# A hand-ordered attention and feed-forward block on one core: four edits to the order of its instructions

## The chip, the cores and the metric

The kernel runs on one core of a Trainium2 chip. The metric is the device time of one execution in microseconds (us). Times of several executions are given as their median; the profile is one further execution that the hardware profiler recorded.

The engines that matter here: PE (TensorE) multiplies matrices into PSUM, PEld is its weight load; DVE (VectorE) does elementwise work and reductions; ACT (ScalarE) does activations and copies; POOL (GpSimd) does elementwise work on SBUF and issues the transfers of raw weights; SP issues the other transfers. Each engine takes its instructions strictly in the order in which the program issues them.

## What is computed

The input x has 4 batches of 512 tokens with 512 features. Cut to what matters, in plain form:

```
q = rotary(x @ Wq + bq)            # 16 heads of 32
k = rotary(x @ Wk + bk); v = x @ Wv + bv      # one head, shared by all 16
x = layernorm(x + softmax(q k' / sqrt(32)) v @ Wo + bo)
w1, w2, w3 = round(w / mean|w|) clipped to -1, 0, 1
x = layernorm(x + (sigmoid(x w1') * (x w2')) w3')     # inner width 1408 = 11 * 128
```

All in 32-bit floats, to about that precision. Where the kernel uses the faster float32r multiplication it keeps a value as two halves, a rounded head and the rest (the tail), and multiplies both.

## The kernel before

**Work and its tiles.** A batch is cut into 4 quarters of 4 heads (`c`), and each quarter's attention into 4 chunks of 128 keys (`t`). That gives 64 attention steps `n = (b, c, t)`. A step issues the scores `ps` (8 matmul records of q and k, and 4 that add the negated row maxima `negm`), the exponentials `es` on ScalarE, the product `acc` with v of the step before, and for batch 0 the sums `den`; for later batches POOL adds the exponentials up in `total`, and `den` is formed once for a quarter. Row maxima are found 7 steps ahead (`LEAD`): `pmax` on PE, then the reduction `mx` on DVE; `spread` transposes them (`pm`), negates them (`m`), writes them to memory (`rows`) and reads them back spread over partitions (`negm`).

**The order.** Everything is pinned to program order. Around the fixed parts of a step the function `Fill` draws pieces of other work from generators: `project_in` (k, v and q of a batch, a half of 4 matmul records a piece), `project_out` (the output projection, the layernorm and the transposes `pt` into the feed-forward's input `y`) and `feed_forward`. Each piece yields its length in us; `draw` takes pieces until the step's pace is used up. A yield of 0 means "not yet", and the other list is asked. Small jobs that come later wait in the list `late`, each with the slot from which its next piece may go; `due` walks that list in order, two times a step, and so the order of the list is the order of those pieces on each engine, SP's transfers among them.

**The opening** (`now < 0`, the first 48 us): the projections of batch 0, the maxima of the first 7 steps and, at its end, k of batch 1. The rotation of q and k is done by `turn` (line 229). In its form `apart`, ScalarE copies the biased product to SBUF (`r`), DVE forms `a` (product with the cosine), and the generator pauses; its second half (shuffle, product with the sine, sum) is issued when the piece after it is drawn, and the sum for the last 32 partitions is POOL's. In the other form everything is issued at once, on DVE, and the shuffle and the sine's product work in place in the PSUM tile (`pk`, `pq`). Before, batch 0 uses the first form and every other batch the second.

**The feed-forward** runs over 11 slices `f` of the inner width, cut into parts of up to 4 slices. For a slice, `gate` issues 8 matmuls `gu` and the tanh `th`; then 8 matmuls `gu` again, DVE's product `hw`, and, after the next pause, `split`: ScalarE's head `h0` and DVE's tail `h1` (both called `h` in the profile). At the end of a part the products `po` with the third weight follow, 4 chunks `t` of tokens, 2 matmuls for each slice, and DVE adds each to `xt`. All parts but a batch's last have the next part's first `gate` between the last `hw` and the first `po`. In a batch's last part the layernorm's statistics (`st`, `mv`) follow each chunk, and the chunks alternate with the next batch's transposes `pt`, whose results ScalarE and DVE take out as `y`. The last part has 3 slices for batches 0 to 2 and 4 for batch 3. This alternation is called the handover below; there are three.

**Buffers.** The products `gu`, `po`, `pt`, `pq`, `pk`, `pm` share two PSUM buffers (tag `mm`), so each has to be read out before the next but one may start. The scores `ps` and the maxima's `pmax` share two others (tag `sc`).

Of the kernel before, what the change touches and what calls it, by code (L numbers as in the profile page):

```python
# [9 lines left out]
F32 = mybir.dt.float32  # L10
F32R = mybir.dt.float32r
# [3 lines left out]
ALU = mybir.AluOpType  # L15
# [4 lines left out]
P = 128  # L20
# [7 lines left out]
def postln_block(  # L28
# [16 lines left out]
    B, T, D = x.shape  # L45
    NC = D // P
    NT = T // P
    NF = wf.shape[1]
# [9 lines left out]
    hp = ctx.enter_context(tc.tile_pool(name="hp", bufs=8))  # L58
# [5 lines left out]
    ps_mm = ctx.enter_context(tc.tile_pool(name="ps_mm", bufs=2, space=PSUM))  # L64
# [188 lines left out]
    def project_in(b):  # L253

        s = batches[b]
        n = P - HD
        while now < NC * NT * (b - 2):
            yield 0

        pk = ps_mm.tile([P, T], F32, tag="mm", name="pk")  # L260
        for c in range(NC):
            mm(pk, wkv_sb[:, c, :], s.xT[c], c == 0, c == NC - 1)
            if c == 1:
                yield -1.8
        kv = work.tile([P, T], F32, tag="kv", name="kv", bufs=1)
        act.activation(kv[n:P], pk[n:P], AF.Identity, bias=bkv_sb[n:P, 0:1])
        s.kT = work.tile([P, T], F32, tag="kT", name="kT", bufs=3)
        rotation = turn(
            [(s.kT[0:n], slice(0, n)), (s.kT[n:P], slice(0, HD))],
            pk, bkv_sb[:, 0:1], bkv_sb[:, 1:2], n, b == 0,  # L270
        )
        next(rotation)
        yield 1.8
        next(rotation, None)
        if b > 0:
            late.append((slot + 2, split_k(b)))
        for c in range(NC):

            while b + 1 == B and c + 2 >= NC and not batches[0].projected:
                yield 0  # L280
            pq = ps_mm.tile([P, T], F32, tag="mm", name="pq")
            for d in range(NC):
                mm(pq, wq_sb[c][:, d, :], s.xT[d], d == 0, d == NC - 1)
                if d == 1:
                    yield -1.8
            if b == 0:

                if c == 0:
                    room = work.tile([P, NC, T], F32, tag="y0", name="room", bufs=1)
                q = s.q[c] = room[:, c, :]  # L290
            else:
                q = work.tile([P, T], F32, tag="q", name="q")
            rotation = turn(
                [(q, slice(0, P))], pq, bq_sb[:, c : c + 1], bq_sb[:, NC + c : NC + c + 1], P, b == 0
            )
            next(rotation)
            if c == 0:
                pv = ps_mm.tile([P, NT, HD], F32, tag="mm", name="pv")
                for t in range(NT):
                    transpose(pv[:, t, :], kv[n:P, ts(t, P)], ident[n:P, n:P])  # L300
                s.v = work.tile([P, NT, HD], F32, tag="v", name="v", bufs=3)
                act.copy(s.v, pv)
            if b > 0:
                late.append((slot + 2, store_q(b, c, q)))
                s.done = c + 1
            yield 1.8
            next(rotation, None)
            s.done = c + 1
        load_xT(NC if b == 0 else 2)

# [9 lines left out]
    def store_q(b, c, q):  # L320
        q2 = work.tile([P, 2, T], F32R, tag="q2", name="q2")
        halves(q2[:, 0, :], q2[:, 1, :], q)
        yield
        whole = dram.tile([P, T], F32, tag="qw", name="qw", bufs=B * NC)
        parts = dram.tile([NG, 2, HD, T], F32R, tag="qp", name="qp", bufs=B * NC)
        move(whole, q)
        for i in range(NG):
            move(
                parts[i].rearrange("n r t -> r n t").bitcast(F32), q2[ts(i, HD)].bitcast(F32)
            )  # L330
        batches[b].qd[c] = (whole, parts)
        yield
# [196 lines left out]
    def split(head, tail, whole):  # L529

        act.copy(head, whole)
        dve.tensor_tensor(tail, whole, head.bitcast(F32), ALU.subtract)
# [41 lines left out]
    def feed_forward(b):  # L574

        s = batches[b]
        mv = small.tile([P, NT, 2], F32, tag="mv2", name="mv2")
        after = [(m, f) for f in range(NF) for m in range(2)][3:]

        short = NF % 4 if b + 1 == B else 0  # L580
        ends = sorted({0, NF, *range(short, NF, 4)})
        parts = [range(*pair) for pair in zip(ends, ends[1:])]
        w3 = [[] for _ in parts]
        th = {}

        def product(k, m):
            w = s.w.pop(0).rearrange("p (c m) -> p c m", c=NC)
            if after:
                s.w.append(load_weight(*after.pop(0)))
            if len(w3[k]) < len(parts[k]):  # L590
                w3[k].append(load_weight(2, parts[k][len(w3[k])]))
            g = ps_mm.tile([P, T], F32, tag="mm", name="gu")
            for c in range(NC):
                for i, part in enumerate(s.y):
                    mm(g, w[:, c, :], part[:, c, :], c == 0 and i == 0, c == NC - 1 and i == 1)
            return g

        def gate(k, f):

            th[f] = work.tile([P, T], F32, tag="th", name="th")  # L600
            act.activation(th[f], product(k, 0), AF.Tanh, scale=0.5)
            if b + 1 == B and f + 1 == NF:

                root = small.tile([P, 1], F32, tag="row", name="root")
                act.activation(root, eps_t, AF.Sqrt)

        for k, fs in enumerate(parts):
            h = []
            for f in fs:
                if f not in th:  # L610
                    gate(k, f)
                    yield 1.9
                up = product(k, 1)
                hw = work.tile([P, T], F32, tag="hw", name="hw")
                dve.scalar_tensor_tensor(hw, th[f], 1.0, up, ALU.add, ALU.mult)
                s.y_done = f == NF - 1
                yield 1.9
                h.append([hp.tile([P, T], F32R, tag="h", name=f"h{i}") for i in range(2)])
                split(*h[-1], hw)
            if fs[-1] + 1 < NF:  # L620
                gate(k + 1, fs[-1] + 1)
                yield 1.9
            for t in range(NT):

                while fs[-1] + 1 == NF and b + 1 < B and 0 <= batches[b + 1].transposed <= t:
                    yield 0
                po = ps_mm.tile([P, D], F32, tag="mm", name="po")
                for n, w in enumerate(w3[k]):
                    for i in range(2):
                        mm(  # L630
                            po,
                            h[n][i][:, ts(t, P)],
                            w,
                            n == 0 and i == 0,
                            n == len(fs) - 1 and i == 1,
                        )
                dve.scalar_tensor_tensor(s.x[t], po, 0.5, s.x[t], ALU.mult, ALU.add)
                if fs[-1] + 1 == NF:
                    stats(s.x[t], mv, t)
                    if b + 1 == B:  # L640
                        for done in range(max(t - 1, 0), t if t + 1 < NT else NT):
                            for _ in layernorm(s.x[done : done + 1], mv[:, done : done + 1, :], True):
                                pass
                            late.append((slot + 1, store(b, done)))
                    elif t == NT - 1:
                        late.append((slot + 1, layernorm(s.x, mv)))
                yield 0.24 * 2 * len(fs)
        if b + 1 < B:
            for t in range(NT):
                late.append((slot + 6, store(b, t)))  # L650
# [58 lines left out]
    late = []  # L709
    slot = 0  # L710
# [21 lines left out]
    def find_maxima(k, *chunks):  # L732

        if k >= len(steps):
            return
        b, c, i = steps[k]
        if chunks[0] == 0:
            ask(k + HEADS)
            while batches[b].done <= c or (b and k not in heads):
                if batches[b].done <= c:  # L740
                    fill.one()
                else:
                    due()
                    ask(k)
        if b == 0:
            row_maxima(b, c, i, chunks[0] // 2)
        else:
            maximum(b, c, i, chunks, heads[k])
        if i == NG - 1 and chunks[-1] == NT - 1:
            late.append((slot + (1 if now < 0 else 2), spread(b, c)))  # L750

    def feed(b):
        fill.urgent.append(project_out(b))
# [122 lines left out]
```

## Time and profile before

| what | value |
|---|---|
| three executions | 702.5, 702.6, 697.24 us; median 702.5 |
| profiled execution | 699.91 us, its span 698.1 us |
| PE busy | 668.9 us, 96% of the span |
| DVE, ACT, POOL busy | 394.0, 290.1, 323.6 us |
| mean granted TensorE clock | 0.986 of full speed |
| chain that ended last | PE 84%, DVE 8%, DMA 2%, ACT 2%, issue 2%, POOL 1% |

The span runs from the first to the last instruction; 1.8 us of the execution lie around it. The granted clock is the share of its full speed at which TensorE was allowed to run. "Waits" are told as engine, waiting instruction, and what ended the wait, with the total in us, the number and the longest.

### The profile page before, as it was taken

The numbers are of one execution on the slowest core, as the hardware profiler recorded it, in microseconds if no ns is written. First come the engines' busy times: TensorE is split into PE (matmuls) and PEld (weight loads), VectorE is DVE, ScalarE is ACT, GpSimd is POOL, SyncE is SP. The second block draws the span as 40 slices with busy tenths as digits, with TensorE's granted clock in tenths as the row PEclk, the third lists the DMA queues.
The fourth block names the chain that finished last, engine by engine and source line by source line (L and its number), as shares of the span: only waits on it lengthen the run. The fifth ranks groups of instructions, "written<-read, shape, count | busy, mean of one in ns | idle before, by whom it ended". The sixth has DMA issues, their size and how long they took to land.

```text
span 698.1 us, 9545 instructions
## 1 busy us (share of the span) xinstructions
PE 668.9 (96%) x3318; PEld 362.2 (52%) x3318; DVE 394.0 (56%) x570; ACT 290.1 (42%) x453; POOL 323.6 (46%) x413
## 2 busy tenths in 40 slices
PE   8989999999979999999999999999998999999995
PEld 6323333443323345665456565654455676768884
DVE  1885676587846675655555764555534433454435
ACT  2454646555424554434334445243434431224213
POOL 0623333435888694657555373666573812202000
PEclk9997999999999999999999999999999999999998
DMA  8662767488648258446213338351130474235631
GB/s 281 242 217 59 239 192 243 134 284 277 197 135 253 93 164 264 121 131 175 77 51 105 113 122 253 93 182 44 52 101 24 137 220 142 68 113 180 191 112 61
DMA packets 59663, 107.20 MB, mean 154 GB/s; under 512 B 13664, under 2 KB 14176, under 8 KB 59616
## 3 DMA queue, kind: packets, MB, share of 16 engines
q1 hardware_dynamic: 51696, 80.65, 37.7%
q0 software_dynamic: 7920, 25.96, 11.3%
q8 instruction: 26, 0.43, 0.3%
q14 instruction: 21, 0.17, 0.1%
HBM read 83.76 MB, written 22.81 MB: 153 GB/s over the span
## 4 chain that ended last, share of the span: by engine, by line
PE 84%; DVE 8%; DMA 2%; ACT 2%; issue 2%; POOL 1%; SPq 1%; ACTq 0%; DVEq 0%; POOLq 0%
PE gu L79 24%; PE po L79 19%; PE ps L79 12%; PE pmax L79 8%; PE acc L79 8%; PE pq L79 6%; PE den L79 4%; DVE mx L74 3%; PE pk L79 1%; DVE xt L74 1%; PE warm L79 1%; ACT es L74 1%; DMA rden<-flat 1%; POOL total L74 1%; DMA xt<-in_x 1%
## 5 line engine op out<-in xcount | busy, mean ns | idle before, releaser
L74 DVE TENSOR_REDUCE mx<-pmax 128x1 f32<-128x512 f32 (+1 forms) x159 | 158.6, 1009 | 113.5 <-PE pmax L79 113.3
L74 ACT ACTIVATE es<-ps 128x1024 f32<-128x1024 f32 x128 | 124.2, 1022 | 154.5 <-PE ps L79 154.5
L79 PE MATMUL gu<-y,wg 128*128 128x512 f32 x704 | 173.2, 395 | 1.3 <-DVE xt L74 0.7
L79 PEld LDWEIGHTS gu<-y,wg 128*128 128x128 f32 x704 | 130.9, 188 | 40.5 <-issue 6.9
L74 POOL TENSOR_TENSOR total<-total,es 128x512 f32<-128x512 f32 x96 | 123.6, 1319 | 47.1 <-ACT es L74 47.1
L79 PE MATMUL po<-wd,h 128*128 128x512 f32 x352 | 90.5, 402 | 6.1 <-DVE h L74 2.6
L74 POOL TENSOR_TENSOR total<-es 128x512 f32<-128x512 f32 x48 | 60.5, 1291 | 69.4 <-ACT es L74 69.4
L79 PEld LDWEIGHTS po<-wd,h 128*128 128x128 f32 x352 | 65.5, 190 | 29.2 <-DVE xt L74 4.3
L79 PE MATMUL pmax<-kr,qr 128*128 128x512 f32 x192 | 75.0, 453 | 2.2 <-ACT es L74 1.6
L79 PE MATMUL acc<-es,v 128*32 128x512 f32 x512 | 68.2, 605 | 0.0
L79 PEld LDWEIGHTS pmax<-kr,qr 128*128 128x128 f32 x192 | 33.7, 188 | 56.1 <-issue 21.4
L74 DVE SCALAR_TENSOR_TENSOR hw<-th,gu 128x512 f32<-128x512 f32 x44 | 30.3, 688 | 56.6 <-PE gu L79 54.9
L74 ACT CAST h<-hw 128x512 fp32r<-128x512 f32 x44 | 27.3, 622 | 82.0 <-DVE hw L74 81.9
L74 DVE SCALAR_TENSOR_TENSOR xt<-po,xt 128x512 f32<-128x512 f32 x48 | 33.2, 692 | 49.7 <-PE po L79 49.6
L79 PE MATMUL ps<-negm,ones_r 2*128 2x512 f32 x256 | 59.0, 787 | 2.0 <-DMA negm<-rows 2.0
L79 PE MATMUL po<-wo_sb,ctxT 128*128 128x512 f32 x128 | 59.1, 594 | 0.3 <-DVE hw L74 0.3
L74 POOL DMA_DIRECT2D raw<-in_wf x66 | 36.1, 549 | 49.0 <-DMA w<-raw 28.2
L74 DVE TENSOR_TENSOR h<-hw,h 128x512 fp32r<-128x512 f32 x44 | 42.6, 968 | 26.3 <-ACT h L74 25.9
L79 PE MATMUL ps<-qT,kT 32*128 32x512 f32 x384 | 55.7, 640 | 0.0
L79 PE MATMUL pq<-xT,wq_sb 128*128 128x512 f32 x112 | 53.0, 601 | 1.0 <-ACT v L74 1.0
L74 ACT ACTIVATE th<-gu 128x512 f32<-128x512 f32 x44 | 26.3, 598 | 45.5 <-PE gu L79 45.4
L79 PEld LDWEIGHTS po<-wo_sb,ctxT 128*128 128x128 f32 x128 | 23.9, 189 | 23.5 <-issue 21.1
(93 smaller groups left out, 630.3 us busy)
## 6 DMA issues: line engine op xcount, KB each, us to landing
wg<-w SPq DMA_DIRECT2D x88, 256.0 KB
raw<-in_wf POOLq DMA_DIRECT2D x66, 256.0 KB, 4.8
qr<-qp SPq DMA_DIRECT2D x96, 128.0 KB
wd<-w SPq DMA_DIRECT2D x44, 256.0 KB
w<-raw POOLq DMA_DIRECT2D x33, 256.0 KB, 4.9
qp<-q SPq DMA_DIRECT2D x48, 128.0 KB
rden<-flat SPq DMA_DIRECT2D x64, 64.0 KB
xt<-in_x SPq DMA_DIRECT2D x16, 256.0 KB
```

What stands on the lines that cost most here:

```text
L74: return lambda *args, **kw: pin(getattr(self.engine, name)(*args, **kw))
L79: pin(nc.tensor.matmul(out, lhsT=lhsT, rhs=rhs, start=start, stop=stop))
```

## The change

Four edits.

1. **Rotation.** `turn` takes the form `apart` whenever it is called in the opening (`now < 0`) and not only for batch 0. Since q may then not be complete before the pause, `store_q` is put on the list after the pause, for the slot after the one in which the generator resumes, and not before it for the slot after the next; `s.done` is set after the pause only.
2. **Heads.** The tiles for a slice's `h` are allocated before the pause. For the last slice of a part ScalarE's head is issued at once behind `hw`; for the others after the pause, as before. The tail is issued after the pause in each case.
3. **Chunks in twos.** In a batch's last part the first two chunks are one piece: the matmuls of all slices but the last for both, then those of the last slice for both, then for each chunk the sum and the statistics. The other two chunks are single as before. The piece waits until two of the next batch's transposes have been issued, where the first chunk waited for one; its length is yielded as that of two.
4. **Maxima's transfers.** `spread` is put at the front of `late`, and so its transpose and its transfers `rows` and `negm` go ahead of whatever else is due in the same slot.

```diff
-            pk, bkv_sb[:, 0:1], bkv_sb[:, 1:2], n, b == 0,
+            pk, bkv_sb[:, 0:1], bkv_sb[:, 1:2], n, now < 0,
...
-                [(q, slice(0, P))], pq, bq_sb[:, c : c + 1], bq_sb[:, NC + c : NC + c + 1], P, b == 0
+                [(q, slice(0, P))], pq, bq_sb[:, c : c + 1], bq_sb[:, NC + c : NC + c + 1], P, now < 0
...
-            if b > 0:
-                late.append((slot + 2, store_q(b, c, q)))
-                s.done = c + 1
             yield 1.8
             next(rotation, None)
+            if b > 0:
+                late.append((slot + 1, store_q(b, c, q)))
             s.done = c + 1
...
+                h.append([hp.tile([P, T], F32R, tag="h", name=f"h{i}") for i in range(2)])
+                if f == fs[-1]:
+                    act.copy(h[-1][0], hw)
                 yield 1.9
-                h.append([hp.tile([P, T], F32R, tag="h", name=f"h{i}") for i in range(2)])
-                split(*h[-1], hw)
+                if f < fs[-1]:
+                    act.copy(h[-1][0], hw)
+                dve.tensor_tensor(h[-1][1], hw, h[-1][0].bitcast(F32), ALU.subtract)
...
-            for t in range(NT):
-                while fs[-1] + 1 == NF and b + 1 < B and 0 <= batches[b + 1].transposed <= t:
+            ahead = NT // 2 if fs[-1] + 1 == NF else 1
+            for some in [range(ahead)] + [(t,) for t in range(ahead, NT)]:
+                while fs[-1] + 1 == NF and b + 1 < B and 0 <= batches[b + 1].transposed <= some[-1]:
                     yield 0
-                po = ps_mm.tile([P, D], F32, tag="mm", name="po")
-                for n, w in enumerate(w3[k]):
+                pos = {t: ps_mm.tile([P, D], F32, tag="mm", name="po") for t in some}
+                last = len(fs) - 1
+                for t, n in [(t, n) for t in some for n in range(last)] + [(t, last) for t in some]:
                     for i in range(2):
                         mm(
-                            po,
+                            pos[t],
                             h[n][i][:, ts(t, P)],
-                            w,
+                            w3[k][n],
...
-                dve.scalar_tensor_tensor(s.x[t], po, 0.5, s.x[t], ALU.mult, ALU.add)
-                if fs[-1] + 1 == NF:
+                for t in some:
+                    dve.scalar_tensor_tensor(s.x[t], pos[t], 0.5, s.x[t], ALU.mult, ALU.add)
+                    if fs[-1] + 1 < NF:
+                        continue
                     stats(s.x[t], mv, t)
...
-                yield 0.24 * 2 * len(fs)
+                yield 0.24 * 2 * len(fs) * len(some)
...
-            late.append((slot + (1 if now < 0 else 2), spread(b, c)))
+            late.insert(0, (slot + (1 if now < 0 else 2), spread(b, c)))
```

## The prediction

> **What bounds the kernel.** I read the page first, then the waits of PE, then the order of time in the four places that the edits touch.
>
> ```profile
> PE 668.9 (96%) x3318; PEld 362.2 (52%) x3318; DVE 394.0 (56%) x570; ACT 290.1 (42%) x453; POOL 323.6 (46%) x413
> PEclk9997999999999999999999999999999999999998
> PE 84%; DVE 8%; DMA 2%; ACT 2%; issue 2%; POOL 1%; SPq 1%; ACTq 0%; DVEq 0%; POOLq 0%
> ```
>
> PE is the bound: 96% busy, 84% of the chain that ended last. No edit removes a matmul, so only two things can be won: time in which PE stands, and time in which its clock is low (the 7 in the fourth slice of the second line). The waits of PE that the edits touch:
>
> ```profile
> PE po L79 <- DVE h L74: 2.6, 4, 1.2
> PE ps L79 <- DMA negm<-rows: 2.0, 1, 2.0
> PE den L79 <- POOL total L74: 1.8, 4, 1.3
> PE ps L79 <- DVE mx L74: 1.7, 1, 1.7
> ```
>
> They are 8.1 us, 1.2% of the span, and each lies in one or a few places.
>
> **Edit 1, the rotation.** In the opening only one rotation of another batch than 0 is issued: that of batch 1's k (`pk`). The half of `pq` after it is completed in step 0, when `now` is 0. So one rotation changes. In order of time, before:
>
> ```profile
> 44.82 0.74 DVE L74 SCALAR_TENSOR_TENSOR a<-pk,bkv_sb,cos_sb 96x512 f32<-96x512 f32 x1
> ...
> 46.01 1.98 PE L79 MATMUL pq<-xT,wq_sb 128*128 128x512 f32 x4
> ...
> 47.00 1.38 DVE L74 TENSOR_TENSOR kT<-a,pk 96x512 f32<-96x512 f32 x2
> 48.40 2.36 DVE L74 TENSOR_REDUCE mx<-pmax 128x2 f32<-128x1024 f32 x2
> 49.69 2.03 PE L79 MATMUL ps<-room,kT 32*128 32x512 f32 x6 [1.69 <-DVE mx L74]
> ```
>
> The shuffle (0.69), the sine's product (0.75) and two sums (1.38) stand on DVE ahead of two maxima of 2.36; the first scores wait for their PSUM. After, only `a` stands ahead: the maxima run from about 45.8 to 48.1 and the second half behind them. ScalarE gets one copy `r` more (0.69 by its row), so the mean `gamma`, for which `pq` waits, comes 0.7 later: `pq` 46.7 to 48.7, `ps` at 48.7 instead of 49.69. Term: -1.0; it is -1.7 if `pq` does not wait for `gamma`, and 0 if the maxima come no earlier. The last 32 partitions of k go to POOL (1.70 by the row of batch 0's k); behind them stand three loads of raw weights, some 5 us later, first needed in step 1. Cost 0 while that step's sign on ScalarE still finds its tile; about 1 if not.
>
> The larger thing is the clock. In these stretches of 1 us the granted clock is the third number from the right:
>
> ```profile
> 49.00:50.00 1.00, 0.32 (x2) 0.30 (x4) 1.00 (x2) 0.00 (x0) 0.00 (x0) 1.00 0.00 0
> 51.00:52.00 1.00, 1.00 (x8) 0.46 (x7) 0.00 (x0) 0.00 (x0) 0.00 (x0) 0.59 0.00 0
> 60.00:61.00 1.00, 1.00 (x9) 0.66 (x12) 0.55 (x1) 0.00 (x0) 0.00 (x0) 0.50 0.00 0
> ```
>
> From 51.2 to 61.5, 10.3 us long, PE runs at half its clock, and this begins just behind the wait. The same happens once more: half clock from 535.9 to 539.3, behind two waits for `h` in the second handover. I take it that the waits bring it on. Steps 0 and 1 take 10.66 (`ps` at 49.69 and 60.35) and 8.10 (68.45). At full clock step 2 takes 6.36 (74.81), and step 1's part from `acc` at 62.36 on, at full clock, took 6.1; with 1.3 for its scores that is 7.4. So step 2 would begin at 48.7 + 6.36 + 7.4 = 62.5 instead of 68.45: edit 1 gives **-6.0**, 1.0 of it the wait and 5.0 the clock. Bounds: -6.8 (both steps at 6.36) and +0.7 (only the longer ScalarE queue is left).
>
> The Trainium skill says in "TensorE: Matmul & The Clock Gate", section "Part 1: The HAM clock gate", that half clock follows an idle window of some 3.4 us, that the window runs freely, and that a busy one releases it. The durations here (10.3 and 3.4) fit three windows and one; the wait of 1.7 is shorter than a window, and by that rule it would not close the gate. Then edit 1 gives only the wait, and the sum below is 5.0 higher.
>
> **store_q** (ScalarE's copy 0.61, POOL's tail 1.27, SP's `qw` 0.42 and `qp` 2.26) moves with the pause. By the generators' order, 7 of 12 quarters come one slot later (steps 0 to 15, one piece a step), the other 5 one slot earlier. Later: 0, since their first reader comes 10 or more slots after; without that, SP would stand 1.3 behind POOL. One that comes earlier costs: in step 16 the copy now stands ahead of `es` and waits for q, which DVE ends at 171.3 where `es` began at 170.66; `es`, and `pmax` behind it, 1.3 later, of which 0.9 shows on PE, because `pk` waits for a transfer at 173.80 anyway.
>
> **Edit 4, the maxima's transfers** (transpose, two small `m`, `rows` 0.38, `negm` 1.08 on SP). One place waits:
>
> ```profile
> 183.78 2.26 SPq L82 DMA_DIRECT2D qp<-q  x4
> ...
> 187.73 2.01 SPq L82 DMA_DIRECT2D rden<-flat  x4
> 189.78 1.08 SPq L82 DMA_DIRECT2D negm<-rows  x2
> ...
> 194.83 1.28 POOL L74 TENSOR_TENSOR ctxT<-ctxT,rden 128x512 f32<-128x512 f32 x1 [5.08 <-DMA rden<-flat]
> 194.96 0.51 PE L79 MATMUL ps<-negm,ones_r 2*128 2x512 f32 x4 [1.99 <-DMA negm<-rows]
> ```
>
> `negm` passes `rden`, so PE's 2.0 go. But POOL waits for `rden`, which is now 1.08 later, and behind `ctxT` in POOL's queue stand `xt` and `total`, for which `den` on PE waits next (198.6). Against that, `qw` and `qp` of the quarter that moved forward (2.7) leave SP ahead of both. PE's next wait is then `total`, about 1.2 earlier than before, less the 0.9 of step 16. Term for both: **-0.3**, from -2.0 (the whole wait) to +2.4 (`rden` 1.1 later, POOL's tail of q 1.27 ahead of `total`). Elsewhere no `negm` ended a wait of PE: 0.
>
> **Edits 2 and 3, the heads and the pair.** In parts that are not a batch's last, the next `gate` covers head and tail (8 `gu`, 1.8), and no wait of `po` lies there: 0; the head in front holds `es` only if `hw` ends after `ps`, at most 0.6. What remains is the ends of four batches. The third handover, where nothing but these generators runs:
>
> ```profile
> 619.74 0.69 DVE L74 SCALAR_TENSOR_TENSOR hw<-th,gu 128x512 f32<-128x512 f32 x1 [1.56 <-PE gu L79]
> 620.10 0.59 ACT L74 CAST y<-pt 128x512 fp32r<-128x512 f32 x1 [1.59 <-PE pt L85]
> 620.48 1.43 PE L79 MATMUL po<-wd,h 128*128 128x512 f32 x5 [0.41 <-DVE hw L74]
> ...
> 622.07 0.50 PE L79 MATMUL po<-wd,h 128*128 128x512 f32 x1 [0.15 <-DVE h L74]
> ```
>
> Before, PE goes through `pt po` four times and reaches the next `gu` at 629.75; the wait for `h` is only 0.15 here. After, the order is `pt pt po+po pt po pt po`, and ScalarE takes the head first. Head 620.5 to 621.1; the two `y` copies follow (0.59 each), DVE has `y` out at 622.4, the tail at 623.1, the second `y` at 623.8. The pair holds both PSUM buffers: first `po` at 622.4, the second only at 623.8, the last slice's matmuls (0.23 each) to 625.6. DVE then does sum, two statistics, sum, two statistics (3.2 in all) before it can take out the third `pt`; `gu` comes at 631.85. Term **+2.1**; between 0 (if PE finds other buffers free) and +3.8 (one more stretch of 3.4 at half clock).
>
> In the same way, the first handover (387 to 405, with maxima on DVE): head and tail no longer hold PE (1.04 before), but the second `po` starts at 391.85 and `den` waits 0.5 for a maximum behind the pair's statistics; the scores of step 45 come at 401.35 instead of 400.14: **+1.2** (-1 to +2.9). The second (527 to 546) is where the edits fit: ScalarE took the head only after `es` (533.02), the tail ended at 535.35. In front of `es` the head ends at 530.5, the tail at 532.8; PE's 2.5 of waits and the 3.4 at half clock go, a wait of 1.25 for the second `y` comes; `gu` at 543.9 instead of 546.16: **-2.3** (-3.5 to 0). At the very end `h` held PE 0.8, but DVE's chain of sums and statistics (1.87 a chunk) leads to the last store, and its first sum moves from 685.40 to about 685.95, as the first chunk is completed behind the second's matmuls; 0.2 of that is absorbed: **+0.35** (-0.4 to +0.6).
>
> **Sum:** -6.0 - 0.3 + 2.1 + 1.2 - 2.3 + 0.35 = -4.95. Against the profiled execution's 699.91 (span 698.1 and 1.8 around it) that is **695.0**. The median shown, 702.5, lies 2.6 above the profiled one, and another run at 697.24 below it; the half clock costs about 5 where it occurs, which would account for such a spread. 1% of the median is 7.0, about what a measurement of this kernel can tell from no change, so the bounds are 695.5 and 709.5.
>
> **Rivals.** *The clock stays low at the start* (another gap closes the gate, or the wait was not its cause): -1.0 in place of -6.0, 700.0. For it: ScalarE still holds `pq`, and gaps of 0.3 to 0.7 remain. Against it: the low stretch begins only at the largest gap. The Trainium skill's rule on the clock gate, told above, is this case. *More is won*: the third handover costs nothing, the `negm` wait goes whole: 695.0 - 2.1 - 1.7 = 691.2, and 690.4 with edit 1's better end. For it: the handover's cost hangs on the two shared buffers as I worked them out. *The pair starves PE* (slower): with both buffers held, PE stands for about 4.5 of 12 us in the third handover and some 3 in the first, and the clock falls there as it did at 51.2, for 10.3 us at about 5 lost each; this decides from the point where half of a 3.4 us stretch is idle. Then the first costs 6.2, the third 7.1, the second gives nothing, edit 1 its 1.0: 699.91 - 1.0 - 0.3 + 6.2 + 7.1 + 0.35 = 712.3. Against it: in the second handover the low stretch lasted 3.4.
>
> **Chances.** Forecast 0.52, its own range 691 to 699 (0.33 of it below 695.5); low clock stays 0.17; more is won 0.13; starved PE 0.18. Faster 0.33 + 0.13 = 0.46, same 0.19 + 0.17 = 0.36, slower 0.18. The range 689 to 708 leaves out the starved case and little else.
>
> **What would show it.** Right: granted clock 1.0 from 45 to 65 and `ps` of step 2 near 62; no `ps` waiting for `negm`; `po` waiting for `h` under 0.5 in sum; `gu` after the third handover 2 later, after the second 2 earlier, relative to the handover's start. Wrong: half clock after 48 us, PE waiting for `y` or `xt` by more than 5 in sum at the handovers, or `den` waiting longer for `total`.

## The result, and the profile after

| what | before | after |
|---|---|---|
| median beside each other | 699.97 us (10 executions, 697.24 to 702.6) | 696.06 us (10 executions, 692.34 to 697.98) |
| profiled execution, its span | 699.91 us, 698.1 us | 697.18 us, 695.4 us |
| mean granted clock | 0.986 | 0.985 |

The ratio is 0.9936, 95% interval 0.9915 to 0.9957: 0.6% faster, between the forecast of 695.0 and no change. In the two profiled executions the difference is 2.7 us, where the sum had 4.95.

The page of the kernel after, its engines, its clock in 40 slices and its chain that ended last:

```profile
PE 665.0 (96%) x3318; PEld 362.4 (52%) x3318; DVE 393.1 (57%) x569; ACT 290.5 (42%) x454; POOL 324.6 (47%) x414
PEclk9999999999989989999999999999999999999998
PE 85%; DVE 9%; ACT 3%; issue 1%; DMA 1%; POOL 0%; DVEq 0%; ACTq 0%; POOLq 0%
```

The 7 in the fourth slice is gone, but there are new 8s in slices 12 and 15, and the mean clock is no higher than before. The chain has 1 point more of PE, DVE and ACT each, and 1 less of DMA, POOL and issue each. The waits of PE (us in total, times, longest) after:

```profile
PE pmax L79 <- ACT es L74: 8.9, 14, 2.6
PE po L79 <- DVE y L74: 3.3, 4, 1.2
PE po L79 <- DVE xt L74: 2.7, 6, 0.9
```

The four waits that were shown of before (`h`, `negm`, `total`, `mx` of the first scores) have gone from the head of this list. `pmax` waiting for `es` is the surprise: before it was 2.3 us in 10 waits, the longest 0.7. To place it, the start of each step's first `ps` on PE is read out of both traces; what a stretch gained or lost is the change of that difference. The whole account of after against before, in us:

| stretch | difference | forecast |
|---|---|---|
| start of the profile to `ps` of step 2 | -7.06 | -6.0 |
| step 17 to 18 (`store_q` earlier) | +0.96 | with the next row -0.3 |
| step 20 to 21 (`negm`, `total`) | -1.0 | |
| step 25 to 28 | +3.3 | 0 |
| first handover, step 43 to 45 | +0.63 | +1.2 |
| second handover, step 61 to 62 | -2.75 | -2.3 |
| third handover, first `pt` to next `gu` | +3.0 | +2.1 |
| end | +0.13 | +0.35 |

The sum is -2.8. These are single profiles, so each row also holds whatever the clock did there in the two of them. The first row in order of time, the kernel after:

```profile
44.50 0.75 DVE L74 SCALAR_TENSOR_TENSOR a<-pk,bkv_sb,cos_sb 96x512 f32<-96x512 f32 x1
45.16 2.34 DVE L74 TENSOR_REDUCE mx<-pmax 128x2 f32<-128x1024 f32 x2
45.49 1.99 PE L79 MATMUL pq<-xT,wq_sb 128*128 128x512 f32 x4
...
47.41 1.13 PE L79 MATMUL ps<-room,kT 32*128 32x512 f32 x6
...
48.91 0.69 DVE L74 TENSOR_TENSOR kT<-a,w 96x512 f32<-96x512 f32 x1
48.96 1.76 POOL L74 TENSOR_TENSOR kT<-a,w 32x512 f32<-32x512 f32 x1 [8.38 <-DVE w L74]
```

The maxima now follow `a` directly, the scores start with no bracket (no wait) as soon as `pq` is done, and the rest of the rotation lies behind. The missed row, steps 25 and 26, first in the kernel before, where the copy of q comes behind `es`:

```profile
247.59 1.94 ACT L74 ACTIVATE es<-ps 128x1024 f32<-128x1024 f32 x2 [1.59 <-PE ps L79]
...
250.15 0.62 ACT L74 CAST q<-q 128x512 fp32r<-128x512 f32 x1
```

and in the kernel after:

```profile
241.91 0.69 DVE L74 TENSOR_TENSOR q<-a,pq 128x512 f32<-128x512 f32 x1
...
242.63 0.62 ACT L74 CAST q<-q 128x512 fp32r<-128x512 f32 x1 [3.73 <-DVE q L74]
243.16 1.93 ACT L74 ACTIVATE es<-ps 128x1024 f32<-128x1024 f32 x2
...
244.22 0.88 PE L79 MATMUL pmax<-kr,qr 128*128 128x512 f32 x2 [1.85 <-ACT es L74]
```

ScalarE's copy of q, which `store_q` issues, is now one slot earlier and stands ahead of `es`. It waits until DVE has rotated q; ScalarE is idle for 3.73 us, the last 2.1 of them with the scores for `es` ready (their last matmuls, 0.80 from 239.71, ended at 240.5), `es` comes late, and `pmax`, which takes the PSUM buffer that `es` empties, waits 1.85. The windows of 2 us (the second number is PE's busy time, the third from the right the granted clock) show what follows:

```profile
50.00:52.00 2.00, 2.00 (x9) 0.62 (x10) 0.94 (x1) 1.99 (x5) 2.00 (x4) 1.00 0.13 16
...
190.00:192.00 2.00, 1.33 (x4) 0.68 (x6) 0.07 (x1) 2.00 (x3) 2.00 (x2) 0.51 0.89 216
...
244.00:246.00 2.00, 1.77 (x7) 1.42 (x7) 0.41 (x1) 1.57 (x4) 2.00 (x3) 0.67 0.90 363
```

At the start the clock is full where it was half before; half clock now lies from 190.1 to 196.9, from 244.7 to 251.5 and from 616.7 to 620.1. The same collision stands at 190: the copy of q waits 5.23 for q, and `pmax` behind it 2.60 for `es`.

The third handover, the kernel after, in order of time:

```profile
614.57 0.62 ACT L74 CAST h<-hw 128x512 fp32r<-128x512 f32 x1 [1.95 <-DVE hw L74]
...
615.09 1.07 ACT L74 CAST y<-pt 128x512 fp32r<-128x512 f32 x2
...
616.45 4.61 PE L79 MATMUL po<-wd,h 128*128 128x512 f32 x12 [1.21 <-DVE y L74]
...
621.38 0.66 PE L85 MATMUL pt<-ident,xt 128*128 128x128 f32 x4 [0.32 <-DVE xt L74]
...
622.90 1.66 PE L79 MATMUL po<-wd,h 128*128 128x512 f32 x6 [0.86 <-DVE xt L74]
...
626.86 1.42 PE L79 MATMUL gu<-y,wg 128*128 128x512 f32 x5
```

The head goes ahead of the `y` copies, so the pair waits for `y` (1.21); the pair's 12 matmuls are one run, and behind it PE waits for both sums. Half clock lies over 3.4 us of this. From the first `pt` at 613.58 to `gu` it is 13.28, where before it was 10.28.

### The profile page after: what moved, and what is told of

Its sections match the earlier page's. It is cut to its first block, busy times and chain, and to the rows that moved or that the text cites. A ratio compares the mean times of both kernels' runs of the same rounds, so it can differ in the third digit from the quotient of the medians.

```text
span 695.4 us, 9548 instructions
## 1 busy us (share of the span) xinstructions
PE 665.0 (96%) x3318; PEld 362.4 (52%) x3318; DVE 393.1 (57%) x569; ACT 290.5 (42%) x454; POOL 324.6 (47%) x414
## 4 chain that ended last, share of the span: by engine, by line
PE 85%; DVE 9%; ACT 3%; issue 1%; DMA 1%; POOL 0%; DVEq 0%; ACTq 0%; POOLq 0%
PE gu L79 24%; PE po L79 19%; PE ps L79 12%; PE pmax L79 9%; PE acc L79 7%; PE pq L79 6%; PE den L79 4%; DVE mx L74 3%; ACT es L74 2%; DVE xt L74 2%; PE pk L79 1%; PE warm L79 1%; DMA xT<-in_xT 1%; DVE st L74 1%; DVE pq L74 1%
## 5 line engine op out<-in xcount | busy, mean ns | idle before, releaser
L79 PE MATMUL po<-wd,h 128*128 128x512 f32 x352 | 89.1, 402 | 6.0 <-DVE y L74 3.3
L79 PE MATMUL pmax<-kr,qr 128*128 128x512 f32 x192 | 76.4, 461 | 8.2 <-ACT es L74 7.9
```

The costliest lines, as they stand in the source:

```text
L79: pin(nc.tensor.matmul(out, lhsT=lhsT, rhs=rhs, start=start, stop=stop))
```

## The experiments

Each kernel was timed beside the kernel before; its ratio and interval are against that. Differences by stretch are from its profiled execution, as in the table above.

**The rotation undone, and the rotation alone.** The first is the kernel after with this edit:

```diff
-            pk, bkv_sb[:, 0:1], bkv_sb[:, 1:2], n, now < 0,
+            pk, bkv_sb[:, 0:1], bkv_sb[:, 1:2], n, b == 0,
```

> The changed kernel with edit 1's form of the rotation undone (batch 1's k is rotated at once, in PSUM, as before); edits 2 to 4 and the later store_q stay. Theory (the rotation's second half ahead of the maxima makes PE wait for 1.7 us, and that wait brings on half clock for some 10 us): step 2's scores begin near 68.5 again instead of 61.4, half clock from about 51 to 61; 7 us slower than the changed kernel, so about 703, and slower than before by 4, since all that is left of the change costs 4.3 in the steps of the profile. Rival (the low clock at the start came by chance in the profiled execution of before, and the wait alone counts): 1.7 to 2.3 slower than the changed kernel, 698.

The second is the kernel before with the reverse edit and nothing else.

> The kernel before with only the rotation of batch 1's k in two halves. Theory: all of edit 1's gain and none of the losses: steps from 2 on 7.1 earlier in the profile, full clock from 45 to 65, 693 where before has 700. Rival (gain needs the later store_q or the maxima's transfers in front as well; or chance of the clock): 698 to 700.

Measured: undone 700.44 (ratio 1.0018, 0.9997 to 1.0040), alone 694.11 (0.9905, 0.9881 to 0.9928). So edit 1 alone gains at least as much as the whole change (0.9936; the intervals overlap), and the other edits together show no gain. Undone came out some 4 us above the kernel after, not the 7 that were expected. With the rotation undone the old wait is back, and half clock behind it, from 52.2 to 59.0:

```profile
48.51 1.83 PE L79 MATMUL ps<-room,kT 32*128 32x512 f32 x6 [1.69 <-DVE mx L74]
...
54.83 3.78 PE L79 MATMUL pq<-spare,wq_sb 128*128 128x512 f32 x4
```

Four `pq` matmuls take 3.78 there and 1.99 at full clock. The start of a profile also varies by itself: with the rotation undone step 2 came 2.1 earlier than before, and in the eight kernels that have the new rotation 6.6 to 7.7 earlier (mean 7.2). Against the mean of before and the undone kernel (1.05) that is 6.1, so the -7.06 of the table holds about 1 of chance.

The undone kernel shows one thing more. Behind the opening its order is that of the kernel after, and at step 20 `pmax` waits for `es` as long; but there its clock stayed full. First the kernel after, then the undone one:

```profile
190.67 1.22 PE L79 MATMUL pmax<-kr,qr 128*128 128x512 f32 x2 [2.60 <-ACT es L74]
191.82 3.75 PE L79 MATMUL den<-total,ones 128*32 128x512 f32 x8
```

```profile
196.69 0.73 PE L79 MATMUL pmax<-kr,qr 128*128 128x512 f32 x2 [2.59 <-ACT es L74]
197.35 2.07 PE L79 MATMUL den<-total,ones 128*32 128x512 f32 x8
```

Against before, step 20 to 21 is 1.0 shorter in the first and 3.8 shorter in the second. So 2.8 of that place is half clock in the one profile and not in the other.

**store_q before the pause again**, in the kernel after:

```diff
+            if b > 0:
+                late.append((slot + 2, store_q(b, c, q)))
+                s.done = c + 1
             yield 1.8
             next(rotation, None)
-            if b > 0:
-                late.append((slot + 1, store_q(b, c, q)))
             s.done = c + 1
```

> The changed kernel with store_q put on the list before the pause, for the slot after the next, as before; everything else as changed. Theory (in the five quarters that come a slot earlier ScalarE's copy of q stands ahead of the exponentials and waits for q's rotation; PE waits for the exponentials, at step 26 long enough to bring half clock): the 3.3 lost between steps 25 and 28 and the 1.0 at step 17 come back, PE's waits of pmax for es fall from 8.9 to under 4, and the 1.0 won at step 20 may go again: 692 to 693 where the changed kernel has 696. Rival (those losses come from the maxima's transfers in front, or from the clock by chance): 696, unchanged.

Measured 694.86 (0.9923, 0.9899 to 0.9948). The two places behave as expected: step 17 to 18 lost nothing (-0.2) and step 25 to 28 gained 0.3 instead of losing 3.3; `pmax` waited for `es` 2.5 in all instead of 8.9. The time is above what was expected, because another place lost: step 20 to 21 by 1.7, where after had won 1.0. So 694.86 and the 696.06 of the kernel after are not told apart: the intervals of their ratios overlap. The waits of PE in that kernel, and below them those of the kernel with the rotation alone:

```profile
PE den L79 <- POOL total L74: 4.6, 1, 4.6
```

```profile
PE ps L79 <- DMA negm<-rows: 2.5, 1, 2.5
PE den L79 <- POOL total L74: 0.7, 1, 0.7
```

With the transfers in front, the scores no longer wait for `negm`, but `den` waits the longer for POOL's `total`, which stands behind `ctxT` and its transfer `rden`: 4.6 in place of 2.5 + 0.7. Both kernels had half clock from 191 to 198, and the one with the rotation alone also lost 1.0 at this step.

**The maxima's transfers in turn**, in the kernel after (`late.append` instead of `late.insert(0, ...)`):

> The changed kernel with the maxima's transfers appended to the list as before; all else as changed. Theory (the transfers in front take the wait for negm away at step 20, which with qw and qp out of the way is worth 1 to 2; nowhere else does it matter): PE waits for negm again near 190 us, steps from 21 on 1 to 2 later, 697 to 698. Rival (the quarter's transfers that moved forward do it alone): 696, and no wait for negm.

Measured 696.95 (0.9961, 0.9947 to 0.9975), which its interval does not tell from the kernel after. No `ps` waited for `negm`: with `store_q` one slot earlier, the q transfers leave SP before `negm` is due in either order, as the rival had it.

**One wait filled.** The kernel before, with seven products of 128 columns that nobody reads ahead of the first scores, where PE stood for `mx`; the rotation as before.

```diff
+        if n == 0:
+            idle = ps_acc.tile([P, P], F32, tag="acc", name="idle")
+            for _ in range(7):
+                mm(idle, ones, ones, True, True)
```

> The kernel before with 7 products of 128 columns that nothing reads, issued on PE just ahead of the first scores, so that PE works through the wait for the maxima; the rotation is as before. Theory (standing still brings on the half clock): the first scores begin at 49.7 as before or up to 0.5 later, but the clock stays full, and steps from 2 on are some 4.5 earlier: 695 to 696. Rival (the fall of the clock has nothing to do with the wait): half clock from about 51 to 61 as before, 700 to 701.

Measured 699.48 (0.9994, 0.9973 to 1.0015). The wait was filled and the clock fell all the same, at 53.8 instead of 51.2. Its timeline and its windows:

```profile
47.43 1.72 PE L79 MATMUL idle<-ones 128*128 128x128 f32 x14
49.29 1.83 PE L79 MATMUL ps<-room,kT 32*128 32x512 f32 x6
...
52.69 2.86 PE L79 MATMUL pmax<-kT,room 32*128 32x512 f32 x8 [0.91 <-ACT es L74]
```

```profile
50.35:53.77 3.42, 2.50 (x16) 0.96 (x16) 0.01 (x1) 2.16 (x3) 0.00 (x0) 1.00 0.00 0
53.77:57.19 3.42, 3.42 (x8) 1.05 (x7) 2.45 (x2) 0.99 (x4) 2.31 (x3) 0.50 0.16 30
```

So filling this one wait does not keep the clock up. In the 3.4 us before the fall PE stood for 0.9, in one gap, and the products that it worked on there (`ps`, `pmax`) use 32 rows of the array or 2.

**All gaps filled.** The same with more such products (7, 3, 5 and 4) in four places of step 0.

> The kernel before with products that nothing reads in four places around the first scores (7 ahead of them, 3 ahead of their second pair, 5 behind them, 4 between the two maxima of step 0), so that PE hardly stands from 47 to 55; no wait is taken away. Theory A (what counts is how much of a stretch of 3.4 PE works, whatever it works on; filling the first wait alone left the other gaps): full clock throughout, steps from 2 on some 4 to 5 earlier, 695 to 696. Theory B (the clock falls for another reason, such as the products of 2 and 32 rows that use little of the array): half clock from about 52 or 54 on for 7 to 10 us, 699.5 to 700.

Measured 699.23 (0.9989, 0.9971 to 1.0007). The clock is full from 46 to 66 (theory A), but the time is near that of theory B; `pq` takes 1.98:

```profile
52.00:54.00 2.00, 2.00 (x18) 1.34 (x12) 0.00 (x0) 1.25 (x2) 0.00 (x0) 1.00 0.00 0
54.00:56.00 2.00, 2.00 (x14) 1.12 (x13) 0.66 (x1) 1.91 (x5) 0.66 (x1) 1.00 0.03 8
```

```profile
52.86 1.38 PE L79 MATMUL idle<-ones 128*128 128x128 f32 x10
...
57.37 1.98 PE L79 MATMUL pq<-spare,wq_sb 128*128 128x512 f32 x4
```

Yet step 2 comes only 1.55 earlier than before, since the fillers lie in PE's own queue: `pmax` starts at 54.17, behind 1.38 of them, where it started at 52.69 with one wait filled. With the gaps filled the clock stays full. But the fillers use all 128 rows, so the run does not tell the gaps from the few rows that the products around them use. Taking the cause of the gaps away wins time, and filling them does not. The 1.55 was lost again on the way (0.26 at step 53): this profile had half clock at 194 to 198, 252 to 256 and 536 to 539.

**Single chunks, and heads after the pause.** The two edits of the handover taken apart, each in the kernel after. First without the pair:

```diff
-            ahead = NT // 2 if fs[-1] + 1 == NF else 1
+            ahead = 1
```

> The changed kernel with every chunk of a batch's last part by itself, as before; the early head and all else as changed. Theory (the pair starves PE at the first and third handover; at the second the early head, not the pair, brings the gain, since the tail then ends before the first chunk needs it): the third handover takes some 10.5 instead of 13.3, the first gives nothing away, the second still wins 2 or more; 692.5 to 693.5 where the changed kernel has 696. Rival (the pair brings the second handover's gain): third and first as before, second without gain; 695 to 696.

Then with the pair, and `act.copy` of the last slice's head behind the pause as for the others:

> The changed kernel with every head after the pause as before; the pair and all else as changed. Theory (the early head is what wins at the second handover): the second handover wins at most 1 instead of 2.75, the third costs 1.5 to 2 (the transposes' copies come first on ScalarE again); 697 to 698. Rival (the pair wins there by itself, since the second chunk's matmuls cover head and tail): second handover unchanged at 2.75, 695 to 696.

Measured: single chunks 691.81 (0.9901, 0.9872 to 0.9931), heads after the pause 695.39 (0.9949, 0.9929 to 0.9969). The length of the three handovers (bounds as in the first table; 12.0 is the third of the kernel with `store_q` before the pause, in which the clock was full there). The second of before holds 3.4 us of half clock, as in all four profiled kernels with late heads and single chunks; the other three rows have none there:

| kernel | first | second | third |
|---|---|---|---|
| before | 17.60 | 10.46 | 10.28 |
| early head, pair (after) | 18.23 | 7.72 | 13.28; 12.0 at full clock |
| early head, single chunks | 17.59 | 6.85 | 11.17 |
| late head, pair | 18.23 | 9.31 | 11.12 |

The early head by itself takes 3.6 from the second handover, the waits for `h` and the half clock together; the pair beside it costs 0.6, 0.9 and 0.8. Heads after the pause won 1.15 in the second and cost 0.84 in the third, where at most 1 and 1.5 to 2 were expected; the time, 695.39, lies below the 697 to 698 expected. In the third the early head costs 0.9 also alone, since it stands ahead of `y` on ScalarE. The second handover before, with the head behind `es`:

```profile
531.20 1.94 ACT L74 ACTIVATE es<-ps 128x1024 f32<-128x1024 f32 x2 [1.06 <-PE ps L79]
...
533.02 0.62 ACT L74 CAST h<-hw 128x512 fp32r<-128x512 f32 x1
...
535.41 0.50 PE L79 MATMUL po<-wd,h 128*128 128x512 f32 x1 [1.22 <-DVE h L74]
```

and with single chunks and the head in front of it:

```profile
524.08 0.62 ACT L74 CAST h<-hw 128x512 fp32r<-128x512 f32 x1 [2.15 <-DVE hw L74]
524.61 0.58 ACT L74 CAST y<-pt 128x512 fp32r<-128x512 f32 x1
...
525.92 1.66 PE L79 MATMUL po<-wd,h 128*128 128x512 f32 x6
```

The first `po` starts with no wait for `h` or `y`.

**The parts joined.** The rotation, `store_q` as before, single chunks, and the early head only in the second handover; first with the maxima's transfers in front, then in turn.

```diff
-                if f == fs[-1]:
+                early = b == 1 and f == NF - 1
+                if early:
                     act.copy(h[-1][0], hw)
                 yield 1.9
-                if f < fs[-1]:
+                if not early:
                     act.copy(h[-1][0], hw)
```

> After, with store_q issued before the pause as in the kernel before, all four chunks single, and the early head only in the handover that showed a gain from it (batch 1's last part); the rotation in the opening and the maxima's transfers in front stay. Theory: the parts add up. Start -7.0 (as in every kernel with the new rotation), step 17 and steps 25 to 28 nothing instead of +0.96 and +3.3, second handover -3.6 (as with single chunks), first and third nothing; at step 20 to 21 between -1.0 and +1.7 (POOL's total, with or without half clock). 699.9 - 7.0 - 3.6 = 689.3, with the place at step 20 688.3 to 691. Rival: the half clock that is removed in one place turns up in another, as it did at step 20 in two kernels: 692 or above, no better than single chunks alone (691.8).

> As the kernel joined from the parts, but with the maxima's transfers in turn as in the kernel before; so only the rotation and one early head are left of the change. Theory: where store_q is as before, edit 4 exchanges a wait of the scores for negm (2.0 to 2.5) for a longer one of den for total (4.6 instead of 0.7 to 1.8), so it is worth nothing within 0.7: 689 to 691. Rival: putting the transfers in front still wins the wait for negm: 2 slower than the joined kernel.

Measured 691.0 (0.9876, 0.9848 to 0.9905) and 689.9 (0.9855, 0.9830 to 0.9879); the intervals overlap. The handovers of the second kernel are 17.57, 6.85 and 10.28, so the parts add up. The wait at step 20 is 3.25 in the first (`den` for `total`) and 2.02 + 1.42 = 3.44 in the second (`ps` for `negm`, then `den`): edit 4 exchanged one wait for another, and nothing of it could be measured. They are 9 and 10 us below before by the medians, and 5 and 6 below the median of the kernel after, which was timed at another time; the interval of the second also lies below that of edit 1 alone.

## Why the prediction was right, and where not

**Edit 1: right in mechanism and size.** -6.0 was forecast; the eight kernels with it against the two without a change there give 6.1 at step 2, and edit 1 alone 5.4 by the medians timed beside each other (699.46 and 694.11). Its profile ends only 4.5 earlier, as 1.5 went again from step 17 to 21, with half clock from 191. Of the -7.06 of the kernel after, 2.28 stands before the first scores and 4.78 between them and step 2; 1.0 and 5.0 were forecast. (The bound of -6.8 for both steps at 6.36 should by its own numbers be -7.0.) Full clock from 45 to 65 was named as the sign, and it is there. `pq` did not wait for `gamma` (45.49 against 45.59 for `gamma`'s start), which was the better bound of the first term. The reason given for the clock, that the waits bring it on, holds only in part: with the one wait of 1.7 filled, the clock fell as well.

The Trainium skill's "TensorE: Matmul & The Clock Gate", section "Part 1: The HAM clock gate", puts half clock, in its table of the two states, behind an idle window of some 3.4 us and lets the window run freely. By that condition the rival of 700.0 would have come; edit 1 alone came to 694.11, so the trace disagrees on it: with one wait filled, PE was busy 2.50 of the 3.4 us before the clock fell at 53.8. It agrees on the length: the stretches of half clock are 6.8 at 190, 6.8 at 244 and 3.4 at 616 in the kernel after, and 6.8 in the kernel with one wait filled.

**store_q: the step that failed.** The prediction costed one of the five earlier quarters, the one of step 16, by looking at what stands behind the copy on ScalarE: 0.9 forecast, 0.96 measured, though 2.0 to 2.2 in three other profiles with the early `store_q` and full clock there. The same look was not taken at the others. In steps 25 and 26 the same collision, `q` late on DVE, the copy ahead of `es`, `pmax` behind `es`, cost 3.3. In the three profiles with the early `store_q` and the transfers in front whose clock stayed full there it cost 1.7, so about half of the 3.3 is the half clock from 244.7. In step 20 it put 2.60 of `pmax` in the place of the waits for `negm` and `total`; that place won 1.0 where the undone kernel, with the same 2.6 at full clock, won 3.8.

So two things were put at nothing: the copy's cost at steps 25 to 28, 1.7, and half clock behind the new waits, some 1.6 there and 2.8 at step 20. With `store_q` back before the pause the 3.3 and the 0.96 went, but step 20 lost 1.7, and the time did not move beyond its interval; what the earlier `store_q` costs in all is not shown.

In the table, `store_q` and edit 4 together are off by 3.6 (3.3 for -0.3), and the other rows by 1.4 the other way, which makes the 2.2 between -4.95 and -2.8. That 696.06 came so near to 695.0 is thus in part luck: the misses cancel in part, and in the undone kernel the same three rows are +2.0, -3.8 and +1.7, in sum -0.1.

**Edit 4: the number near, the reason not shown.** -0.3 was forecast with the earlier `store_q`; the rows up to step 21 sum to 0.0, with half clock in the second. With the transfers in turn and the earlier `store_q` no `ps` waited for `negm` either, so here edit 4 took away nothing that the earlier `store_q` had not. With `store_q` before the pause `total`, named as the next wait, took all of the gain back (4.6 for 3.2).

**Heads and pair: the size was right, the split was not made.** First, second and third: +1.2, -2.3, +2.1 forecast, +0.63, -2.75, +3.0 measured, of the last 1.3 half clock at 616. The -2.75 also holds the 3.4 us of half clock that went, as forecast. The signs `po` not waiting for `h`, `gu` later in the third and earlier in the second held. The prediction costed both edits as one, and so did not see that beside the early head the pair costs in every handover, and that the early head wins in one only.

**The rivals.** PE did not starve as in the slower case: at the three handovers its waits for `y` and `xt` come to 5.4 us, 4.8 of `po` and 0.6 of `pt`. That is above the 5 that the prediction named as a sign of being wrong, and half clock did come, but for one stretch of 3.4 in one handover, not for three in two.

**What stays open.** Which gaps close the clock. In each of the twelve profiles the granted clock changes only at points that lie whole multiples of 3.41 us apart (in the kernel after at 190.05, 196.88, 244.66, 251.49, 616.72 and 620.13), and the points differ from profile to profile. PE's busy time (the second number) in stretches between such points: before, ahead of the fall at 51.2; the kernel after, ahead of no fall and of the one at 190.1; the undone kernel at step 20, ahead of no fall:

```profile
47.77:51.18 3.41, 1.72 (x9) 0.60 (x10) 2.96 (x3) 0.60 (x2) 0.00 (x0) 1.00 0.13 52
```

```profile
46.70:50.11 3.41, 2.45 (x16) 1.02 (x16) 2.83 (x5) 2.88 (x8) 1.15 (x1) 1.00 0.00 0
186.64:190.05 3.41, 1.43 (x16) 0.16 (x8) 2.28 (x5) 0.97 (x2) 3.41 (x4) 1.00 0.60 208
```

```profile
192.11:195.52 3.41, 1.99 (x20) 0.36 (x12) 2.83 (x6) 0.42 (x1) 3.41 (x4) 1.00 0.73 234
```

Of the wait of 2.6 at step 20, 2.0 lies in the one stretch in the kernel after; in the undone kernel a point cuts it into 1.4 and 1.2. So where a wait falls among these points has a part in it, and no edit here set that. Over all twelve profiles no stretch with PE busy for less than 1.6 of the 3.41 kept the full clock, and between 1.6 and 2.1 it went both ways; the prediction's "half of a 3.4 us stretch" is near that. Two falls in step 0 came after stretches of 2.50, all of it products of 32 rows or 2, while the kernel after kept its clock with 2.45, of which 0.8 was `pq` with 128 rows. Whether the rows count beside the time is not shown.

## What to carry to other kernels

When a piece is moved by a slot, look at every place in which it lands, not at the first: a copy of 0.6 us issued ahead of the instruction that empties a PSUM buffer passes the lateness of its own input on (here `pmax` stood 1.85 and 2.60 behind two such copies). Take edits that sit in one place apart before joining them; here the early head alone won 3.6 in a place where the pair gave 0.9 of it back. In an engine bound at 96%, a wait can cost more through the clock than by its length (2.8 us behind a wait of 2.6 at step 20), and whether it does can change from one profile to the next with the same instructions; so read a place in several profiles before its gain or loss is put down to an edit. Remove a wait's cause rather than fill it: here the filler stood on PE's path.

## What the runs showed of the hardware that was not expected

The granted clock changes on a grid of 3.41 us in every profile, so its low stretches came in lengths of 3.4, 6.8 and 10.2 us. It fell after a stretch in which PE stood for only 0.9 of the 3.41 (at 53.8 with one wait filled), and stayed full when the gaps around it were filled with products of 128 rows. The low stretches also move: every profiled kernel without the one at the start had one of at least 3.4 us between 188 and 198, and none of the three with it (before, the rotation undone, one wait filled) had one there.
